# Gathers three tiles apart, slots placed earlier in the window, and a matmul for each gather to wait for

## The chip, the cores and the metric

The kernel runs on one core of a Trainium2 chip. The metric is the device time of one execution in microseconds; lower is better. Names of engines: PE is the matmul engine (PEld its weight loads), DVE the vector engine, ACT the scalar engine, POOL the GpSimd engine, SP the sync engine, which here only issues DMAs.

## What is computed

`x` has 16 batches of 512 tokens with 512 features, in float32. A conditional linear layer with a low-rank part gives g; a router picks 4 of 16 blocks of a feed-forward net for each token; the output is `x` plus the sum of the four blocks' results.

```python
z1 = einsum('bfi,bir->bfr', x, v) / 512
z = einsum('bfr,bor->bfo', z1, u) / 16             # u = v = fside
g = gelu(einsum('bfi,oi->bfo', x, W) + fc_bias + z + cond)
prob = softmax(g @ w_router + b_router)
_, idx = top_k(prob, 4)                            # 4 of 16 blocks for each token
h = relu(einsum('nd,ebd->neb', g, w1b) + b1b)      # block e: 128 hidden units
y = einsum('neb,ebd,ne->nd', h, w2b, mask) + b2
out = x + y
```

## The kernel before

**Lists in DRAM.** The kernel does the feed-forward only for the blocks that a token picked. Each block has a list of slots in DRAM, `g_d`, with room for a row of g in each slot. A token's g is scattered to four slots; tiles of 128 consecutive slots of one list are then computed; the results go to the same slots of `y_d`; and each token's four result rows are gathered back and added to x.

**Stage one, the windows.** `window(b)` runs for the 16 batches. It has eight halves (`cond_half(b, h)`), each with the `pc` matmuls (L261) of half an output quarter; after each second half `gelu` (ACT, L270) makes `gT`. The table `do` lists what is issued behind each half, in the order in which the engines get it, since PE, DVE and ACT follow the program's order: for the next batch `weights` (`pw` matmuls L241, four `we` adds on DVE L243) and `turn_x` (transposes L248, copy `xT` on DVE L250); for the batch before, called `a`, `logits_in` (`pa`, L285), `logits` (`pl`, L294), `route_in` (three small DVE operations and Exp on ACT), `route` (DVE: top 4, one-hot, counts), four `turn_g` (transposes L357, a copy `gr` on DVE L359 or ACT L361), `rank` (`pp` matmuls, L417 to L423) and `place`, which writes `slot`, the row numbers of a batch (L441). For the batch after next it has `spread_v`, `turn_v` and `turn_v_out`. Transposes share two PSUM buffers, `ps_t`; `pa`, `pl`, `pu` and `pp` share two others, `ps_s`. `chores` adds bookkeeping on DVE at halves 1, 3 and 6 of some windows: `fill`, `take`, `count`, `table_part`.

**The scatters.** `put(b, c, j, after)` (POOL, L447) scatters 128 rows of `gr` to the j-th choice's slots. There are 16 for a batch, two behind each half, for the batch two windows back, and each also waits for a matmul of that half. The last two batches' puts, and then five `put_zero` (L500) that fill up the last tile of each list, go into the first steps of stage two.

**Stage two, the tiles.** 271 tiles, one for each step `i`. SP: `fetch(i + 4)` loads `gt` (L631). PE, ACT: `turn(i + 1)` (transposes L649, copy `gs` on ACT L650), `first(i)` (`ph` L656, relu `h` on ACT L660), `second(i - 1)` (`py` L666, copy `y` on ACT L667, store to `y_d` on SP L668). DVE: `pick(i + 2)` copies the block's weights to `wcur` (L643), of which there are three. The first 22 tiles (`AHEAD`) are of full lists and don't wait for later scatters; tile 22 and those behind it wait for all puts and zeros.

**Sums.** A chunk is 128 tokens, 64 in all. `plan` puts its parts in steps: `load_x` (ACT's DMA queue, L689; chunks of the last two batches are still in SBUF) into one of 11 buffers; four `get_y` (POOL, L694), each a gather of 128 rows of `y_d`; then on DVE `sum_b` (L708), two `sum_y` (L712), two `sum_x` (L715); and `store` on SP (L718). `begun(b, c)` is the number of tiles that must be stored before the chunk is complete: 38 for the first five chunks, then 4n + 15 for the n-th. A gather waits for these stores. It also waits for its `yg` tile, of which there are six, for two gathers each. `mark[0]` is the last `ph` matmul issued. The planned step of a chunk's gathers is

```python
at = max(begun(b, c) + GAP, at + TOP_K if b + c else 0)     # GAP = 3, TOP_K = 4
```

so it is 41 for the first chunk, and 4n + 37 for the n-th: 293 for the last, 22 steps after the last tile.

Of the kernel before, what the change touches and what calls it, by code (L numbers as in the profile page):

```python
# [19 lines left out]
TOP_K = 4  # L20
# [5 lines left out]
def adaln_ffn_kernel(  # L26
# [31 lines left out]
    B, S, D = x.shape  # L58
# [3 lines left out]
    NC = S // P  # L62
# [27 lines left out]
    SYNC = mybir.DependencyInfo(mybir.DependencyClass.Sync, mybir.DependencyReason.DATA)  # L90

    def alone(ins):

        tc.declare_no_dep(ins.ins, group="put_g", reason="disjoint rows of the lists")
        tc.declare_no_dep(ins.ins, group="get_g", reason="the tiles that run ahead are full")
        tc.add_to_no_dep_group("put_g", ins.ins)
# [348 lines left out]
    def put(b, c, j, after):  # L445

        ins = nc.gpsimd.indirect_dma_start(  # L447
            out=g_d[:, :],
            out_offset=bass.IndirectOffsetOnAxis(ap=slot[:, b, c, j : j + 1], axis=0),
            in_=grs[b, c].bitcast(I32),  # L450
            in_offset=None,
        )
        tc.add_manual_dep(ins.ins, after.ins.name, SYNC, reason="spread over the products")
        alone(ins)
        if b < Q:
            early.append(ins.ins)
# [42 lines left out]
    def put_zero(i, after):  # L499
        ins = nc.gpsimd.indirect_dma_start(  # L500
            out=g_blocks if i else g_d[:, :],
            out_offset=bass.IndirectOffsetOnAxis(ap=zero_i[:, i : i + 1], axis=0),
            in_=(zero if i else zero[:, 0:D]).bitcast(I32),
            in_offset=None,
            bounds_check=NSLOT // ZB - 1 if i else NSLOT - 1,
            oob_is_err=False,
        )
        tc.add_manual_dep(ins.ins, after.ins.name, SYNC, reason="spread over the products")
        alone(ins)
# [65 lines left out]
    for k in range(known):  # L575
        chores.setdefault(B - 2 + k // 3, []).append(parts_of[k])

    def window(b):
        a = b - 1
        do = [[] for _ in range(2 * ND)]  # L580
        if b + 1 < B:
            do[0] += [(weights, b + 1)]
            do[2] += [(turn_x, b + 1, 0), (turn_x, b + 1, 1)]
            do[4] += [(turn_x, b + 1, 2), (turn_x, b + 1, 3)]
            if b > 0:
                do[1] += [(logits_in, a)]
                do[3] += [(logits, a), (route_in, a)]
                do[4] += [(route, a)]
                do[5] += [(turn_g, a, 0), (turn_g, a, 1)]
                do[6] += [(turn_g, a, 2), (turn_g, a, 3)]  # L590
                do[7] += [(rank, a), (place, a)]
            if b + 2 < B:
                do[2] += [(spread_v, b + 2)]
                do[5] += [(turn_v, b + 2), (turn_v_out, b + 2)]
        else:
            do[0] += [(logits_in, a)]
            do[1] += [(logits, a), (route_in, a)]
            do[2] += [(turn_g, a, 0), (turn_g, a, 1), (route, a)]
            do[3] += [(turn_g, a, 2), (turn_g, a, 3)]
            do[5] += [(rank, a), (place, a)]  # L600
        for h, what in zip((1, 3, 6), chores.get(b, ())):
            do[h] += [what]
        for h in range(2 * ND):
            ins = cond_half(b, h)
            for what, *args in do[h]:
                what(*args)
            if b > 1:
                for j in (0, 1):
                    put(b - 2, h // 2, h % 2 * 2 + j, ins)
            if later:  # L610
                what, *args = later.pop(0)
                what(*args)
# [4 lines left out]
    rows, gts, wcs, gss, hTs, mark, stores = {}, {}, {}, {}, {}, {}, []  # L617
# [59 lines left out]
    def begun(b, c):  # L677

        n = b * NC + c + 1
        return max(AHEAD + E, n * PB // NC + E - 1)  # L680
# [10 lines left out]
    def get_y(b, c, j):  # L691
        if j % 2 == 0:
            ygs[b, c, j // 2] = ygp.tile([P, 2, D], F32, tag="yg", name=f"yg_{b}_{c}_{j}")
        ins = nc.gpsimd.indirect_dma_start(  # L694
            out=ygs[b, c, j // 2][:, j % 2, :].bitcast(I32),
            out_offset=None,
            in_=y_d[:, :],
            in_offset=bass.IndirectOffsetOnAxis(ap=slot[:, b, c, j : j + 1], axis=0),
        )
        new = stores[begun(b, c - 1) if b + c > 0 else 0 : begun(b, c)]  # L700
        tc.declare_no_dep(ins.ins, group="put_y", keep=new, reason="later tiles have no slot of this chunk")
        for p in new:
            tc.add_manual_dep(ins.ins, p.name, SYNC, reason="its rows")
        tc.keep_in_program_order(ins)
        tc.add_to_no_dep_group("get_y", ins.ins)

# [14 lines left out]
    GAP = 3  # L721
# [4 lines left out]
    def plan(step, *what):  # L726
        work.setdefault(step, []).append(what)

    for b in range(B):
        for c in range(NC):  # L730
            at = max(begun(b, c) + GAP, at + TOP_K if b + c else 0)
            k = b * NC + c
            soon = FREE - 2 * XA + 2 * k if k < XA else FREE + 4 + k - XA
            plan(soon if k < XA + XB else max(at - 24, soon), load_x, b, c)
            for j in range(TOP_K):
                plan(at + j, get_y, b, c, j)
            plan(at + LAND, sum_b, b, c)
            for h in range(2):
                plan(at + LAND + 1 + 2 * h, sum_y, b, c, h)
                plan(at + LAND + 2 + 2 * h, sum_x, b, c, h)  # L740
            plan(at + LAND + 4, store, b, c)


    z = B - 1
    for step, *what in (
        (-1, logits_in, z), (0, logits, z), (0, route_in, z), (1, turn_g, z, 0), (1, turn_g, z, 1), (1, route_a, z),
        (2, route_b, z), (2, turn_g, z, 2), (3, route_c, z), (3, turn_g, z, 3), (4, rank, z), (5, place, z),
        (6, count, B // Q - 1), (7, ends), *((8 + k, *w) for k, w in enumerate(parts_of[known:])), (8 + NTC, table, 1),
    ):
        plan(step, *what)  # L750
    for i in range(NC * TOP_K):
        for k, b in enumerate((z - 1, z)):
            plan(8 * k + i // 2, lambda b, c, j: put(b, c, j, mark[0]), b, i // TOP_K, i % TOP_K)
    for i in range(1 + NZ):
        plan(16 + i // 3, lambda i: put_zero(i, mark[0]), i)

    ENG = mybir.EngineType
    with tc.manual_schedule(engines={ENG.PE, ENG.DVE, ENG.Activation}):
# [10 lines left out]
        for b in range(B):  # L769
            if 2 <= b + 2 < B:  # L770
                load(b + 2)
            window(b)
# [76 lines left out]
```

## Time and profile before

| what | value |
|---|---|
| median of 3 runs | 1096.34 us (1089.81 to 1098.36) |
| profiled execution | 1086.83 us, its span 1085.1 us |
| mean granted PE clock | 0.967 |
| busy: PE, DVE, ACT, POOL | 970.9, 648.0, 518.8, 550.3 us |
| DMA | 342.43 MB, 316 GB/s over the span |
| puts (L447), gathers (L694) | 256 each, 993 and 1106 ns on POOL |

The profile page splits the span into 40 slices of 27.1 us and gives the busy share of each engine in tenths. A group's row names line, engine, operation, output and input, count, then busy time and mean duration. A timeline row has the start and the length in us, engine, line, operation and tiles, and in brackets how long the engine had been idle before it and what ended that. A releaser called remote is another core or a queue that the profile doesn't know.

### The profile page before, as it was taken

What the parts mean: (1) busy time and instruction counts of PE and PEld (TensorE: products, weight loads), DVE (VectorE), ACT (ScalarE), POOL (GpSimd) and SP (SyncE); (2) the same over time, 40 slices, a digit from 0 to 9 for tenths busy, and PEclk for the clock granted to TensorE, in tenths of its full rate; (3) what the DMA queues carried; (4) which work ended last, traced back from release to release, by engine and by line L of the source; (5) the groups of instructions that cost most, each with busy time, mean ns of one, the idle gap of its engine ahead of it and who ended that gap; (6) DMA issues with size and microseconds to landing.
All of it is one profiled execution on the core that took longest, in us unless ns stands there. A gap on an engine that the chain in (4) does not pass through costs nothing.

```text
span 1085.1 us, 19007 instructions
## 1 busy us (share of the span) xinstructions
PE 970.9 (89%) x5320; PEld 639.3 (59%) x5320; DVE 648.0 (60%) x1450; ACT 518.8 (48%) x1006; POOL 550.3 (51%) x538
## 2 busy tenths in 40 slices
PE   5998988988999888789799999999999999999960
PEld 3544444544444455567577677677767777777740
DVE  4365667566556767323366666566666666666675
ACT  2333332342333434456466666566656566666640
POOL 2046666666666667500454445455444454444555
PEclk9999999999999988989899999999999999999985
DMA  9966667566654469988799999999999999999996
GB/s 301 332 230 216 224 215 261 208 225 242 226 223 179 170 224 318 358 265 272 259 382 405 394 388 403 391 394 395 395 397 401 395 396 398 380 405 398 392 354 211
DMA packets 161480, 342.43 MB, mean 316 GB/s; under 512 B 28723, under 2 KB 36951, under 8 KB 159046
## 3 DMA queue, kind: packets, MB, share of 16 engines
q1 hardware_dynamic: 110928, 188.53, 48.1%
q0 software_dynamic: 41856, 136.96, 33.6%
q10 hardware_dynamic: 8592, 15.73, 4.1%
q8 instruction: 44, 0.72, 0.3%
q14 instruction: 60, 0.49, 0.1%
HBM read 179.91 MB, written 163.32 MB: 316 GB/s over the span
## 4 chain that ended last, share of the span: by engine, by line
PE 58%; DMA 19%; DVE 8%; issue 5%; ACT 3%; POOL 2%; SPq 2%; another core or an unknown queue 2%; ACTq 1%; DVEq 0%; POOLq 0%
PE pc L261 17%; DMA gt<-g_d 14%; PE ph L656 14%; PE py L666 13%; PE pts L649 6%; PE ptx L248 2%; PE ptg L357 2%; PE pw L241 2%; PE pa L285 1%; ACT gs L650 1%; PE pl L294 1%; DVE xT L250 1%; DMA yg<-y_d,slot 1%; POOL g_d L447 1%
## 5 line engine op out<-in xcount | busy, mean ns | idle before, releaser
L694 POOL DMA_INDIRECT yg<-y_d,slot x256 | 283.1, 1106 | 338.0 <-DVE xr L715 163.8
L643 DVE COPY wcur<-wall 128x1028 f32 x271 | 193.0, 713 | 271.1 <-PE py L666 164.0
L447 POOL DMA_INDIRECT g_d<-gr,slot x256 | 254.3, 993 | 185.2 <-issue 65.8
L656 PE MATMUL ph<-gs,wcur 128*128 128x128 f32 x2168 | 293.7, 279 | 17.7 <-ACT gs L650 9.8
L666 PE MATMUL py<-wcur,h 128*128 128x512 f32 x542 | 281.2, 601 | 5.5 <-ACT h L660 4.8
L656 PEld LDWEIGHTS ph<-gs,wcur 128*128 128x128 f32 x2168 | 266.8, 194 | 26.6 <-ACT gs L650 17.4
L261 PE MATMUL pc<-xT,we 128*128 128x512 f32 x512 | 246.3, 608 | 0.0
L649 PEld LDWEIGHTS pts<-ident,gt 128*128 128x128 f32 x1084 | 134.9, 143 | 165.2 <-issue 108.8
L667 ACT COPY y<-py 128x512 f32<-128x512 f32 x271 | 159.2, 587 | 94.0 <-PE py L666 69.5
L650 ACT COPY gs<-pts 128x512 f32<-128x512 f32 x271 | 160.0, 590 | 85.0 <-DMA gt<-g_d 39.6
L649 PE MATMUL pts<-ident,gt 128*128 128x128 f32 x1084 | 165.6, 276 | 16.4 <-DMA gt<-g_d 14.3
L660 ACT ACTIVATE h<-ph,wcur 128x128 f32<-128x128 f32 x271 | 100.0, 369 | 89.6 <-PE ph L656 43.0
L261 PEld LDWEIGHTS pc<-xT,we 128*128 128x128 f32 x512 | 88.4, 192 | 88.7 <-issue 88.7
L270 ACT ACTIVATE gT<-pc,biasT 128x512 f32<-128x512 f32 x64 | 44.0, 688 | 158.0 <-PE pc L261 101.8
L712 DVE TENSOR_TENSOR yg<-yg 128x512 f32<-128x512 f32 x128 | 87.3, 682 | 8.2 <-DMA yg<-y_d,slot 6.8
L666 PEld LDWEIGHTS py<-wcur,h 128*128 128x128 f32 x542 | 83.2, 194 | 6.8 <-ACT h L660 5.1
L250 DVE COPY xT<-ptx 128x512 f32<-128x512 f32 x64 | 42.0, 686 | 60.4 <-PE ptx L248 27.8
L715 DVE TENSOR_TENSOR xr<-xr,yg 128x512 f32<-128x512 f32 x112 | 76.6, 684 | 0.0
L357 PE MATMUL ptg<-ident,gT 128*128 128x128 f32 x256 | 37.8, 281 | 27.1 <-issue 9.8
L357 PEld LDWEIGHTS ptg<-ident,gT 128*128 128x128 f32 x256 | 30.0, 143 | 50.5 <-issue 24.9
L243 DVE TENSOR_TENSOR we<-pw,wc 128x512 f32<-128x512 f32 x64 | 40.1, 683 | 23.9 <-PE pw L241 16.2
L248 PEld LDWEIGHTS ptx<-ident,x 128*128 128x128 f32 x256 | 31.3, 146 | 18.3 <-issue 14.9
(159 smaller groups left out, 511.2 us busy)
## 6 DMA issues: line engine op xcount, KB each, us to landing
gt<-g_d SPq DMA_DIRECT2D x271, 256.0 KB
y_d<-y SPq DMA_DIRECT2D x271, 256.0 KB
x<-in_x_dram SPq DMA_DIRECT2D x16, 1024.0 KB
xr<-in_x_dram ACTq DMA_DIRECT2D x56, 256.0 KB
out_dram<-xr SPq DMA_DIRECT2D x56, 256.0 KB
wall<-in_w1T_dram SPq DMA_DIRECT2D x16, 256.0 KB
wall<-in_w2T_dram SPq DMA_DIRECT2D x16, 256.0 KB
g_d<-gr,slot POOLq DMA_INDIRECT x256
```

Of the source, the lines that this page charges most:

```text
L261: ins = nc.tensor.matmul(pms[o], lhsT=wes[b][:, k, o * P : (o + 1) * P], rhs=xTs[b, k], start=(k == 0), stop=(k == ND - 1))
L357: nc.tensor.transpose(pt[:, k, :], gTs[b, k][:, c * P : (c + 1) * P], ident)
L447: ins = nc.gpsimd.indirect_dma_start(out=g_d[:, :], out_offset=bass.IndirectOffsetOnAxis(ap=slot[:, b, c, j : j + 1], axis=0), in_=grs[b, ...
L643: nc.vector.tensor_copy(wcs[i], wall_f[:, bass.DynSlice(w, WW)])
L649: nc.tensor.transpose(pt[:, k, :], gts[i][:, k * P : (k + 1) * P], ident)
L650: nc.scalar.copy(gs.rearrange("p k t -> p (k t)"), pt.rearrange("p k t -> p (k t)"))
L656: mark[0] = nc.tensor.matmul(ph, lhsT=wcs[i][:, k * P : (k + 1) * P], rhs=gss[i][:, k, :], start=(k == 0), stop=(k == ND - 1))
L660: nc.scalar.activation(h, ph, AF.Relu, bias=wcs[i][:, ND * P : ND * P + 1])
L666: nc.tensor.matmul(py, lhsT=hTs[i], rhs=wcs[i][:, ND * P + 4 : WW], start=True, stop=True)
L667: nc.scalar.copy(y, py)
L694: ins = nc.gpsimd.indirect_dma_start(out=ygs[b, c, j // 2][:, j % 2, :].bitcast(I32), out_offset=None, in_=y_d[:, :], in_offset=bass.Indir ...
L712: nc.vector.tensor_tensor(yg[:, 0, :], yg[:, 0, :], yg[:, 1, :], ALU.add)
```

## The change

Four things are edited. In `window` the table `do` is one for all windows: `logits_in` of batch `a` moves from half 1 to 0, `logits` and `route_in` from 3 to 1, `route` from 4 to 2, `rank` and `place` from 7 to 4; `turn_g` goes to halves 4, 6, 7 and 7; `weights` from 0 to 3; `turn_x` to halves 1, 5, 5 and 6. The puts run ten behind (`LAG`): in window b the last ten of batch b - 2 and then the first six of batch b - 1, and the last ten of batch 14, the 16 of batch 15 and the zeros take steps 0 to 4, 6 to 13 and 14 of stage two. The chunks come three steps apart until 3n + 38 meets 4n + 18 at the 20th chunk (step 98), and from there `at` is `begun + 3`: 274 for the last chunk. A chunk's four gathers stand at `at`, `at`, `at + 1` and `at + 2`. Last, each gather also waits for `mark[0]`, the `ph` matmul of its step.

```diff
--- before.py
+++ after.py
@@ -575,38 +575,38 @@
     for k in range(known):
         chores.setdefault(B - 2 + k // 3, []).append(parts_of[k])
 
+    LAG = 10
+
+    def puts_of(b, i, after):
+        if b >= 0:
+            put(b, i // TOP_K, i % TOP_K, after)
+
     def window(b):
         a = b - 1
         do = [[] for _ in range(2 * ND)]
-        if b + 1 < B:
-            do[0] += [(weights, b + 1)]
-            do[2] += [(turn_x, b + 1, 0), (turn_x, b + 1, 1)]
-            do[4] += [(turn_x, b + 1, 2), (turn_x, b + 1, 3)]
-            if b > 0:
-                do[1] += [(logits_in, a)]
-                do[3] += [(logits, a), (route_in, a)]
-                do[4] += [(route, a)]
-                do[5] += [(turn_g, a, 0), (turn_g, a, 1)]
-                do[6] += [(turn_g, a, 2), (turn_g, a, 3)]
-                do[7] += [(rank, a), (place, a)]
-            if b + 2 < B:
-                do[2] += [(spread_v, b + 2)]
-                do[5] += [(turn_v, b + 2), (turn_v_out, b + 2)]
-        else:
+        if b > 0:
             do[0] += [(logits_in, a)]
             do[1] += [(logits, a), (route_in, a)]
-            do[2] += [(turn_g, a, 0), (turn_g, a, 1), (route, a)]
-            do[3] += [(turn_g, a, 2), (turn_g, a, 3)]
-            do[5] += [(rank, a), (place, a)]
+            do[2] += [(route, a)]
+            do[4] += [(rank, a), (place, a), (turn_g, a, 0)]
+            do[6] += [(turn_g, a, 1)]
+            do[7] += [(turn_g, a, 2), (turn_g, a, 3)]
+        if b + 1 < B:
+            do[1] += [(turn_x, b + 1, 0)]
+            do[3] += [(weights, b + 1)]
+            do[5] += [(turn_x, b + 1, 1), (turn_x, b + 1, 2)]
+            do[6] += [(turn_x, b + 1, 3)]
+        if b + 2 < B:
+            do[2] += [(spread_v, b + 2)]
+            do[5] += [(turn_v, b + 2), (turn_v_out, b + 2)]
         for h, what in zip((1, 3, 6), chores.get(b, ())):
             do[h] += [what]
         for h in range(2 * ND):
             ins = cond_half(b, h)
             for what, *args in do[h]:
                 what(*args)
-            if b > 1:
-                for j in (0, 1):
-                    put(b - 2, h // 2, h % 2 * 2 + j, ins)
+            for i in range(2 * h, 2 * h + 2):
+                puts_of(b - 2 + (i >= LAG), (i - LAG) % (NC * TOP_K), ins)
             if later:
                 what, *args = later.pop(0)
                 what(*args)
@@ -701,6 +701,7 @@
         tc.declare_no_dep(ins.ins, group="put_y", keep=new, reason="later tiles have no slot of this chunk")
         for p in new:
             tc.add_manual_dep(ins.ins, p.name, SYNC, reason="its rows")
+        tc.add_manual_dep(ins.ins, mark[0].ins.name, SYNC, reason="spread over the products")
         tc.keep_in_program_order(ins)
         tc.add_to_no_dep_group("get_y", ins.ins)
 
@@ -728,12 +729,12 @@
 
     for b in range(B):
         for c in range(NC):
-            at = max(begun(b, c) + GAP, at + TOP_K if b + c else 0)
+            at = max(begun(b, c) + GAP, at + 3 if b + c else 0)
             k = b * NC + c
             soon = FREE - 2 * XA + 2 * k if k < XA else FREE + 4 + k - XA
             plan(soon if k < XA + XB else max(at - 24, soon), load_x, b, c)
             for j in range(TOP_K):
-                plan(at + j, get_y, b, c, j)
+                plan(at + 3 * j // TOP_K, get_y, b, c, j)
             plan(at + LAND, sum_b, b, c)
             for h in range(2):
                 plan(at + LAND + 1 + 2 * h, sum_y, b, c, h)
@@ -748,11 +749,12 @@
         (6, count, B // Q - 1), (7, ends), *((8 + k, *w) for k, w in enumerate(parts_of[known:])), (8 + NTC, table, 1),
     ):
         plan(step, *what)
+    for i in range(LAG):
+        plan(i // 2, lambda i: puts_of(z - 1, i, mark[0]), NC * TOP_K - LAG + i)
     for i in range(NC * TOP_K):
-        for k, b in enumerate((z - 1, z)):
-            plan(8 * k + i // 2, lambda b, c, j: put(b, c, j, mark[0]), b, i // TOP_K, i % TOP_K)
+        plan(6 + i // 2, lambda i: puts_of(z, i, mark[0]), i)
     for i in range(1 + NZ):
-        plan(16 + i // 3, lambda i: put_zero(i, mark[0]), i)
+        plan(14, lambda i: put_zero(i, mark[0]), i)
 
     ENG = mybir.EngineType
     with tc.manual_schedule(engines={ENG.PE, ENG.DVE, ENG.Activation}):
```

## Prediction

> **What bounds the kernel now.** I read the page's slices first, then busy time by stretches, the waits, and the timeline of each engine.
>
> ```profile
> PE   5998988988999888789799999999999999999960
> POOL 2046666666666667500454445455444454444555
> DMA  9966667566654469988799999999999999999996
> GB/s 301 332 230 216 224 215 261 208 225 242 226 223 179 170 224 318 358 265 272 259 382 405 394 388 403 391 394 395 395 397 401 395 396 398 380 405 398 392 354 211
> ```
>
> A slice is 27.1 us. Up to slice 15 (stage one, the windows) PE is busy and DMA is not full. From slice 21 on PE and DMA are both at 9 and the rate stays near 396 GB/s. In the last slices PE is gone: a tail of POOL, DVE and DMA.
>
> ```profile
> 459.00:486.00 27.00, 20.66 (x126) 16.23 (x127) 5.58 (x8) 12.54 (x26) 0.00 (x0) 0.83 0.76 248
> 513.00:540.00 27.00, 19.06 (x106) 14.03 (x105) 8.30 (x13) 10.74 (x23) 13.10 (x14) 0.81 0.78 260
> 702.00:729.00 27.00, 26.47 (x169) 19.91 (x168) 17.48 (x27) 16.98 (x36) 13.29 (x12) 1.00 1.04 393
> 1053.00:1080.00 27.00, 0.00 (x0) 0.00 (x0) 18.46 (x29) 0.00 (x0) 18.07 (x17) 0.50 0.85 271
> ```
>
> These stretches (PE, PEld, DVE, ACT, POOL busy, then clock, DMA share, GB/s) show three places where PE loses time besides the full-DMA stretch: about 460, about 525, and after 1053. The start of each tile's relu (ACT L660, in ACT's timeline) numbers the tiles: tile 0 at 393.18, 20 at 455.73, 21 at 468.23, 41 at 512.10, 43 at 518.27, 44 at 529.75, 270 at 1048.06. Where nothing disturbs, one tile takes 2.19 us (22 to 42): PE's own pace. From 74 to 242 it takes (986.28 - 596.92) / 168 = 2.318 us.
>
> ```profile
> PE ptg L357 <- issue: 7.9, 5, 1.8
> PE ptg L357 <- DVE gr L359: 7.4, 4, 2.1
> PE ptg L357 <- ACT gr L361: 2.8, 1, 2.8
> ```
>
> These are PE's waits in 100 to 343 us (total, times, longest): in stage one nearly all are at the transposes of g (L357).
>
> **Stage one: the new order in a window.** From rank matmul to rank matmul (L423) windows 2 to 14 take 22.9, 24.6, 22.2, 25.3, 24.9, 22.2, 23.3, 25.3, 22.4, 23.6, 23.7, 25.2 and 24.0 us, 309.6 together. The shortest three, less the 0.8 to 1.0 us that PE waits in each, give 21.4 us of work, so 31 us are lost. The loss has one form: the third and fourth `turn_g` (half 6) need a `ps_t` buffer whose copy `gr` (DVE) stands behind `route`, 4.35 us of DVE work issued at half 4 (334.94 to 339.28).
>
> I walk one new window with the rows of the old one, from the start of half 0: 1.8 us for the four pc matmuls of a half, pa 1.0, pl 0.8, four transposes 0.44, pw 1.1, rank 0.3. pa ends at 2.8 and pl at 5.4; `route_in` (three ops of 0.22) 6.2; Exp, with its table load of 1.28 behind gelu at half 1, 7.0; `route` on DVE 7.1 to 11.4; PE comes to `rank` at 12.35, 0.9 later, so no wait. The `we` adds take DVE to 13.9, `place` to 15.45. The next users of `ps_t`: `turn_g(0)` at 12.65 wants the first `we` add (12.1); `turn_x(1)`, `turn_x(2)` at 14.9 and 15.35 want 12.7 and 13.8; `turn_g(1)` at 18.05 wants 16.1; `turn_g(2)`, `turn_g(3)` at 20.75 and 21.2 want 19.3 and 20.0. Nothing waits. I take 0.3 us for each of the seven plain windows, where 12.9 are lost now: -10.8.
>
> In the six windows with chores (5, 6, 7, 9, 13, 14) the move costs something: `count` at half 1 (4.1 us of DVE, 231.62 to 235.83) now stands before `route`, so acc comes at about 15.3 and `rank` waits 2.9 us; a `table_part` (2.5 us) does the same in smaller. I charge 2.2 to 3 us each, 16.7, where 18.5 are lost now: -1.8. Window 15 gets a `rank` wait of 2.3 us, but PE waits there 2.23 us for `wcur` before its first tile anyway: 0. **Stage one: about -12**; bounds 0 (every margin missed) and -25 (no chore window waits).
>
> **The scatters into stage two.** A put is 0.97 us and 0.30 between two, 1.27. Six puts of the last batch but one now go out in window 15, POOL having 20.4 us of puts per window, under its length. After stage one 10 + 16 + 5 DMAs remain instead of 32 + 5. The last puts are gated by steps 6 to 13, the zeros by step 14 (440.9). `slot` of the last batch is written at 414.2, before step 6 (415.9). So the zeros start at 441.3 instead of 448.31, 7 us sooner.
>
> ```profile
> 453.96 1.05 POOL L500 DMA_INDIRECT g_d<-zero,zero_i  x1 [0.31 <-issue]
> 465.34 1.09 PE L649 MATMUL pts<-ident,gt 128*128 128x128 f32 x4 [10.14 <-DMA gt<-g_d]
> ```
>
> The last zeros land at 462.5; SP then issues gt of tile 22, and its transposes stop waiting: the 12.5 us between tiles 20 and 21. At most 10.3 can go. DMA is full there (share 1.0 from 441 to 453), and six puts of 262 KB less at 370 GB/s are 4.2 us. **I take -5**, between 0 and -10.
>
> **The gathers, from tile 41 on.** Now POOL issues twelve gathers in a row (512.3 to 527.5) until the six `yg` tiles are full.
>
> ```profile
> 529.74 0.70 DVE L643 COPY wcur<-wall 128x1028 f32 x1 [9.36 <-remote]
> 529.75 0.37 ACT L660 ACTIVATE h<-ph,wcur 128x128 f32<-128x128 f32 x1 [6.53 <-remote]
> ```
>
> Behind the burst tiles 43 and 44 take 3.98 and 11.48 us: 11.1 lost. The releaser is unknown; it stands nowhere else at that length, so I tie it to the burst. With a product of its own step for each gather there is no burst, and the 11.1 go (they are in the sum below). Behind a waiting gather POOL has only more gathers; who waits for them is DVE's sums.
>
> Against that stand bytes. A tile moves 0.262 MB of gt and as much of y; each gather 0.262, each xr load and out store 0.262 per chunk. One chunk per four tiles makes 0.918 MB, over 2.318 us 396 GB/s: the limit. From steps 41 to 98 a chunk now comes every three tiles.
>
> - Before: 41 to 61 (no xr loads) 20 x 2.19, the loss 11.1, 61 to 237 176 x 2.318, then no loads, 33 x 2.19: 535.2 us. The trace has 535.96.
> - After: 41 to 50 at 2.21 and out stores from 48, 20.3; 50 to 74 with 1.049 MB, 24 x 2.648 = 63.6; 74 to 98 with 1.027 MB, 24 x 2.593 = 62.2; 98 to 218 as now, 278.2; the loads end 19 steps sooner, 52 x 2.19 = 113.9. Sum 538.2: **+3**.
>
> The Trainium skill ("DMA: Bandwidth & Descriptors", Where 436 GB/s comes from) speaks otherwise on both sides: the ports give 435 GB/s, while for HBM to SBUF some 358 per core bind. By 435 the stretch 98 to 218 would be PE's (2.19), and the difference -2; by 358 it is +5. The row of 396 is between and decides.
>
> Two waits are added. (a) An xr load goes to one of 11 buffers, and is planned 24 steps ahead. With chunks 33 steps apart instead of 44 over 11 chunks it comes 9 steps after the old owner's gathers, 2 after its out store. That store is issued about 2.5 us after its step's relu and lands some 7 us later (605.35, 7.02 in the chain), so ACT, at 6.8 us, stands about 2.7 us in front of the load; gs of the next tiles is queued behind it, and PE for gs. gs has 1.3 us of slack (514.0 against 515.34). Some ten loads: 0 if the full DMA hides it, 14 beyond the slack, 27 with none. I take +4, near the low end, as PE waits 0.4 us per tile for gt there anyway.
>
> (b) From step 98 on a gather stands three steps behind its last tile. That tile's y leaves 2.3 us after the relu of the next step; gt in the same queue lands in 6.6 to 8.4 us when DMA is full, so the stores are there 2.4 us after the gather's own product. POOL then starts two gathers, the second 3.7 us after that relu. The sum that reads them stands on DVE at 10.9 (four steps, and 1.6), before the copies of `wcur`, for which PE waits. So 7.2 us are left for landing. Rows: 4.4 to 5.8 in the tail, when 271 to 354 GB/s flow; gt's 8.4 at the other end. The same page (Arbitration) has each DMA engine go round its rows by packets, so gathers, in a row of their own, don't queue behind SP's; I take 5.5, nearest the tail's, and 0 for the wait. At 8.4 it is 1.2 us, of which 1.1 is slack.
>
> **The tail.** Now from relu 270 to the end 37.0 us: 21 gathers at 1.3 and the last one's way out. After, eight gathers are left; those of the last chunk wait for y of tile 270: issued at 2.7, landed 5.2 later (the way from about 507 to 512.3 that the first gather waits for today), 7.9; four gathers, last start 11.8, landed 16.9; two adds 18.3; store 3.7 (1081.4 to 1085.1): 22.0. **-15.**
>
> **Sum:** -12 - 5 + 3 + 4 - 15 = **-25**. The profiled execution (span 1085.1, time 1086.83) would take 1061.8. It ran 9.5 below the median 1096.34; on that I forecast **1071**. A measurement of this kernel can tell about 1% from no change.
>
> **Rivals.**
> 1. The waits are only moved (within 1%, chance 0.17): stage one gives 3 for 12, since `rank` now stands close behind `route`, the scatters' stall is DMA's (0), and ACT pays 10 for 4: -3 +3 +10 -15 = -5, 1091. For it: margins of 0.5 to 0.9 us in my walk, full DMA at 447 to 453. Against: three windows of 22.2 to 22.4 today.
> 2. Slower (0.18): sums in wait of gathers. From chunk 20 on, 44 chunks; it begins where a gather lands later than 7.2 + 1.1 = 8.3 us after its start and costs 44 us per us. At 9.2 it is +40: 1071 + 40 = 1111. For it: DVE is in order and `wcur` stands behind; stores to HBM at full DMA could take longer than gt. Against: 4.4 to 5.8 in the tail.
> 3. More (0.10): stage one gives 25 and the scatters 10, ACT nothing: -25 -10 +3 -15 = -47, 1049.
>
> My forecast has 0.55. Faster 0.55 + 0.10, same 0.17, slower 0.18. The likeliest case alone runs from 1055 to 1085; the range, with most of rival 1 and 3 and part of 2, from 1048 to 1106.
>
> **What would show it.** Rank to rank near 21.7 in plain windows and about 24 in those with `count`, no 1.8 us waits at L357; zeros near 7 us sooner against relu 14; no jump at tiles 43 and 44; 2.6 us per tile from 50 to 98 at 396 GB/s; ACT waiting for out stores before L689; no DVE wait for `yg` over 2 us; 22 us from relu 270 to the end. Wrong if tiles 98 to 218 take more than 2.4 us, or windows over 23.

## Result: slower, and by how much depends on the chip

| chip | before | after | ratio (95% interval) |
|---|---|---|---|
| the chip of the times shown above | 1095.48 us (6 runs) | 1135.12 us (6 runs) | 1.0359 (1.0303 to 1.0416) |
| a second chip, later | 1060.21 us (7 runs) | 1076.06 us (4 runs) | 1.0153 (1.0116 to 1.0189) |

The change makes the kernel slower. The forecast was 1071 us, with a range from 1048 to 1106, on the first chip. The experiments met five chips. On one of them before takes about 1094 us, as on the first (it may be the same chip); on the other four 1059 to 1062 us. I call them chips of the first and of the second kind. The trace shows the difference too: in all six traces of the first kind, 9 to 21 waits (27 to 56 us in all) end with a releaser called remote, and in all fourteen of the second kind none does.

The name misleads here. An engine tells another that its work is done by raising a counter, a semaphore, and the trace records each increment. All 93 of these waits end with an increment of one semaphore (117), which only PE's own instructions raise. So no other core stands behind them: PE's signal came later than the end that the profile gives its matmul, and that end is modelled. The six traces also lack 41 to 45% of the increments that the program's DMAs should leave, the fourteen at most 0.5%. So on the first kind the names of releasers are less certain than on the second.

From the start of each tile's relu, the parts of the time are as follows, in us. For before on the second kind I use e4, which differs from it only in what the puts wait for and takes the same time (0.9994).

| part | before, 1st | after, 1st | before (e4), 2nd | after, 2nd | forecast of the change |
|---|---|---|---|---|---|
| start to tile 0 | 393.2 | 437.5 | 377.2 | 387.2 | -12 |
| tile 0 to 41 | 118.9 | 113.2 | 115.9 | 109.0 | -5 |
| 41 to 98 | 141.0 | 150.8 | 131.9 | 150.4 | |
| 98 to 218 | 279.5 | 282.0 | 281.0 | 280.9 | 41 to 270 together: |
| 218 to 270 | 115.4 | 118.3 | 115.7 | 118.1 | +3 +4 |
| tile 270 to the end | 37.0 | 25.3 | 37.6 | 25.2 | -15 |
| span | 1085.1 | 1127.2 | 1059.3 | 1070.8 | -25 |

On the first kind the sum is +44.3 -5.7 +15.2 -11.7 = +42.1; on the second +10.0 -6.9 +20.8 -12.4 = +11.5. What was to be gained at tiles 20 to 22 and in the tail is there. What was lost lies in stage one and in tiles 41 to 98.

The same slices, stretches and lines as shown of before, now from after on the first chip. A slice is 28.2 us here.

```profile
PE   5996988798998879779987999999999999999991
POOL 2046655565666556620354454444544444544443
DMA  9965655574755347978899999999999999999995
GB/s 302 337 209 191 216 183 194 204 247 148 259 209 214 147 153 228 323 280 305 268 358 393 362 397 402 394 391 404 399 387 399 400 390 391 394 398 348 388 354 187
```

Stage one (to slice 15) has one slice at 6 and one at 7 where, behind the first slice, before had only 8 and 9. At the end PE is at 9 until the last slice but one: the tail is shorter.

```profile
498.00:525.00 27.00, 22.64 (x134) 17.05 (x133) 6.29 (x10) 14.06 (x29) 0.00 (x0) 0.94 0.76 260
553.00:580.00 27.00, 22.88 (x141) 17.15 (x140) 14.44 (x22) 14.48 (x31) 15.18 (x15) 0.97 1.01 369
740.00:767.00 27.00, 26.06 (x165) 19.46 (x164) 16.52 (x26) 17.13 (x37) 12.82 (x12) 1.00 1.04 392
1100.00:1127.00 27.00, 3.29 (x13) 1.39 (x12) 10.22 (x16) 2.03 (x5) 9.68 (x10) 0.64 0.56 188
```

The columns are again PE, PEld, DVE, ACT, POOL busy, clock, DMA share, GB/s. PE gets 2 us more in the first stretch (tiles 20 to 22) and nearly 4 more in the second, where the gathers begin; the third is as before. Line by line:

```profile
486.19 0.98 POOL L500 DMA_INDIRECT g_d<-zero,zero_i  x1 [0.31 <-issue]
503.83 1.09 PE L649 MATMUL pts<-ident,gt 128*128 128x128 f32 x4 [4.36 <-DMA gt<-g_d]
555.91 0.70 DVE L643 COPY wcur<-wall 128x1028 f32 x1 [1.49 <-PE py L666]
557.29 0.37 ACT L660 ACTIVATE h<-ph,wcur 128x128 f32<-128x128 f32 x1
```

The last zero stands 5.8 us behind the relu of tile 14, where it stood 13.1 behind; PE's wait at tile 22 falls from 10.14 to 4.36 us. At tiles 43 and 44 no wait of 9.36 and 6.53 us is left. The transposes of g hardly wait in this stretch any more (5.6 us in all, 22.1 before); rank does (PE's waits from 100 to 343 us: total, times, longest):

```profile
PE pp L417 <- DVE acc L350: 15.7, 7, 5.2
PE pw L241 <- DVE xT L250: 3.2, 3, 1.1
PE ptg L357 <- DVE xT L250: 2.9, 2, 1.9
```

### The profile page after: what moved, and what is told of

It is laid out like the page before. It is cut to its first block, busy times and chain, and to the rows that moved or that the text cites. A ratio compares the mean times of both kernels' runs of the same rounds, so it can differ in the third digit from the quotient of the medians.

```text
span 1127.2 us, 19110 instructions
## 1 busy us (share of the span) xinstructions
PE 991.4 (88%) x5320; PEld 648.0 (57%) x5320; DVE 643.8 (57%) x1450; ACT 517.1 (46%) x1006; POOL 539.1 (48%) x538
## 4 chain that ended last, share of the span: by engine, by line
PE 72%; DVE 10%; DMA 9%; issue 4%; ACT 2%; SPq 1%; ACTq 1%; another core or an unknown queue 0%; POOL 0%; DVEq 0%; POOLq 0%
PE ph L656 18%; PE pc L261 18%; PE py L666 17%; PE pts L649 9%; DMA gt<-g_d 4%; DMA out_dram<-xr 3%; PE ptg L357 3%; PE ptx L248 3%; PE pa L285 1%; PE pl L294 1%; ACT gs L650 1%; PE pw L241 1%; DVE ti L326 1%; DVE we L243 1%; DVE xT L250 1%
## 5 line engine op out<-in xcount | busy, mean ns | idle before, releaser
L694 POOL DMA_INDIRECT yg<-y_d,slot x256 | 273.8, 1070 | 357.2 <-DMA y_d<-y 113.1
L643 DVE COPY wcur<-wall 128x1028 f32 x271 | 193.8, 716 | 241.6 <-PE py L666 143.7
L656 PEld LDWEIGHTS ph<-gs,wcur 128*128 128x128 f32 x2168 | 266.6, 194 | 44.9 <-ACT gs L650 29.1
L261 PE MATMUL pc<-xT,we 128*128 128x512 f32 x512 | 252.8, 625 | 0.0
L261 PEld LDWEIGHTS pc<-xT,we 128*128 128x128 f32 x512 | 93.6, 200 | 101.6 <-issue 94.7
L300 DVE TENSOR_TENSOR pr<-pl,br 128x64 f32<-128x64 f32 x16 | 3.6, 225 | 108.7 <-PE pc L261 60.5
L361 ACT COPY gr<-ptg 128x512 f32<-128x512 f32 x32 | 18.6, 583 | 85.0 <-PE ptg L357 74.1
```

The lines of the kernel that those rows point to most:

```text
L261: ins = nc.tensor.matmul(pms[o], lhsT=wes[b][:, k, o * P : (o + 1) * P], rhs=xTs[b, k], start=(k == 0), stop=(k == ND - 1))
L643: nc.vector.tensor_copy(wcs[i], wall_f[:, bass.DynSlice(w, WW)])
L656: mark[0] = nc.tensor.matmul(ph, lhsT=wcs[i][:, k * P : (k + 1) * P], rhs=gss[i][:, k, :], start=(k == 0), stop=(k == ND - 1))
L694: ins = nc.gpsimd.indirect_dma_start(out=ygs[b, c, j // 2][:, j % 2, :].bitcast(I32), out_offset=None, in_=y_d[:, :], in_offset=bass.Indir ...
```

## Experiments

Two theories of stage one came out of the two first traces. **U**: when POOL issues a long unbroken row of puts, releases reach ACT and DVE late. **R1**: the new order makes PE wait at rank, because work on DVE stands ahead of the route. This is what led to U, from after on the first chip; two rows of POOL, one of ACT, one of PE:

```profile
68.86 0.97 POOL L447 DMA_INDIRECT g_d<-gr,slot  x1 [5.34 <-DVE acc L350]
93.21 0.97 POOL L447 DMA_INDIRECT g_d<-gr,slot  x1 [0.30 <-issue]
94.49 0.59 ACT L289 COPY parts<-pa 128x512 f32<-128x512 f32 x1 [13.57 <-remote]
95.13 1.89 PE L294 MATMUL pl<-pick,parts 128*128 128x16 f32 x8 [11.69 <-issue]
```

Twenty puts stand in a row from 68.9 to 94.2. `pa` is complete at 81.5, yet its copy on ACT begins at 94.49, when the row ends; PE stands 11.69 us behind it. In the same window on the second kind (after_again) the copy begins when `pa` ends:

```profile
81.49 0.59 ACT L289 COPY parts<-pa 128x512 f32<-128x512 f32 x1 [2.48 <-PE pa L285]
```

In eleven of the twelve windows that follow in after, the chain from `pa` to `route_in` is late by 0.6 to 3.2 us against after_again.

**e1 to e4 (second kind).** The two halves of the change alone, the old places of the puts in the new window, and a row of puts in the old window.

```diff
 e1 = before
+            at = max(begun(b, c) + GAP, at + 3 if b + c else 0)
+                plan(at + 3 * j // TOP_K, get_y, b, c, j)
+        tc.add_manual_dep(ins.ins, mark[0].ins.name, SYNC, reason="spread over the products")
 e2 = after without these three
 e3 = after
-    LAG = 10
+    LAG = 16
 e4 = before
-            if b > 1:
-                for j in (0, 1):
-                    put(b - 2, h // 2, h % 2 * 2 + j, ins)
+            if b > 1 and h == 0:
+                for j in range(NC * TOP_K):
+                    put(b - 2, j // TOP_K, j % TOP_K, ins)
```

> The kernel before with the gathers' part of the change alone: chunks three tiles apart, and each gather waits for its tile's product. Stage one is that of before, so tile 0's relu should start at 393 us in every theory. If the two traces add up part by part, tiles 41 to 270 take some 551 us instead of 536 and the end behind the last relu 25 instead of 37: the kernel lands at about +3 us, 1099. The rival that the gathers gain by themselves what the prediction gave them (+7 there, -15 at the end) says 1087. If the wait for the product is what hurts, tiles 41 to 270 take over 555 us and it is slower than 1105.

> The changed kernel with the gathers of before (four tiles apart, no wait for a product), so the windows' new order and the puts' new places alone. Both theories of the windows say that tile 0's relu starts at about 437 us, 44 later than before, and that tiles 0 to 41 give 6 back: about 1133 us. If instead the gathers' part carries the loss, this one is at 1100 or less.

> The changed kernel with LAG = 16 instead of 10: the order of work in a window stays new (rank right behind route), but all 16 puts of a batch stand two per half in the window after its slots are known, as before, so GpSimd never waits for slots and then catches up. Theory U (a long unbroken row of puts on GpSimd makes the releases of the scalar and the vector engine late by 1 to 3 us, on the chain from logits to rank): windows of 22 to 23.5 us, tile 0 at 385 to 400 us, total about 1093 (stage one back, tiles 0 to 41 keep or lose the 6 us that the earlier puts gained). Rival R1 (the new order itself lets TensorE wait for the route's sums at rank): windows stay at 24 to 25 us, tile 0 at 425 to 437, total 1125 to 1140.

> The kernel before, with one edit: the 16 puts of a window all wait for the first half's product instead of two for each half, so that GpSimd issues them in one row of some 20 us; nothing else moves. Theory U: the logits of the next batch lie within that row, their releases come 1 to 3 us late in two or three places, and windows grow by 2 to 5 us, tile 0 at 420 to 450 us, total 1120 to 1150. Rival R1 (order of work only): windows unchanged at 22 to 25 us, tile 0 at 390 to 398, total 1090 to 1100.

Before took 1061.4 us here. Measured: e1 1072.5 (1.0106, 1.0053 to 1.016), e2 1064.2 (1.0035, 1.0021 to 1.0049), e3 1085.4 (1.0206, 1.014 to 1.0272), e4 1060.3 (0.9994, 0.9975 to 1.0012). Against my expectation the gathers' part carries most of the loss on this chip: e1's tile 0 is at 376.3, but tiles 41 to 270 take 551.7 us where e4 takes 528.6, and 12.7 come back in the tail. The window part is +10 us at tile 0 (387.7), not +44. And U fails here: e4's puts stand in unbroken rows of 20 us, and its plain windows are 22.2 us all the same. e3, with two puts behind each half again as in before, is no help either; its windows are those of e2.

What is left of the window's loss shows in windows counted from the last gelu of one batch to that of the next (windows 1 to 15, from ACT's timeline, us):

| | 1 | 2 | 3 | 4 | 5 | 6 | 7 | 8 | 9 | 10 | 11 | 12 | 13 | 14 | 15 |
|---|---|---|---|---|---|---|---|---|---|---|---|---|---|---|---|
| e4 (old) | 21.9 | 22.1 | 22.2 | 22.2 | 24.9 | 24.2 | 22.2 | 22.2 | 22.2 | 22.2 | 22.2 | 22.2 | 22.2 | 21.7 | 17.9 |
| e2 (new) | 20.2 | 21.1 | 21.1 | 21.1 | 24.5 | 26.2 | 26.3 | 21.1 | 26.3 | 21.1 | 21.1 | 21.1 | 26.1 | 24.4 | 21.9 |
| e7 (new, chores late) | 20.2 | 21.1 | 21.1 | 21.1 | 21.1 | 21.1 | 21.1 | 23.0 | 21.1 | 22.8 | 21.1 | 21.1 | 21.1 | 22.3 | 18.8 |

The seven plain windows gain 1.1 us each, window 1 gains 1.7: 9.4 together. The seven with chores (5, 6, 7, 9, 13, 14, 15) lose 20. One of them, window 7 of e2, on DVE and then on PE:

```profile
184.48 0.43 DVE L388 TENSOR_TENSOR first_q<-first_q,left 128x256 f32<-128x256 f32 x1
184.83 0.21 DVE L318 TENSOR_REDUCE sm<-ex 128x4 f32<-128x64 f32 x1
188.44 0.77 DVE L350 TENSOR_TENSOR acc<-acc,mask 128x16 bf16<-128x16 bf16 x4
189.26 0.20 PE L417 MATMUL pp<-acc,ones 128*128 128x80 bf16 x1 [2.81 <-DVE acc L350]
190.63 3.30 PE L261 MATMUL pc<-xT,we 128*128 128x512 f32 x4
```

```profile
187.00:189.20 2.20, 0.00 (x0) 0.00 (x0) 1.96 (x10) 0.00 (x0) 1.59 (x3) 1.00 0.48 181
190.60:193.80 3.20, 3.20 (x7) 1.31 (x6) 2.36 (x8) 0.59 (x1) 0.00 (x0) 0.55 0.08 28
```

`count` holds DVE from 180.85 to 184.83, and `route` begins the moment it ends. So rank waits 2.81 us, and that is not all: from 190.6 to 193.8 the granted clock is 0.55, and the four `pc` matmuls that take 1.88 us elsewhere take 3.30. Window 7 is 5.2 us over a plain one: PE stands still for 3.15 us of it, and its work takes 2.03 us longer. This is R1, with a price nearly twice the wait.

**after_again, e5, e6, e7 (second kind).** The changed kernel itself; the spacing without the wait for a product; the sums two steps later; the chores behind rank.

```diff
 e5 = e1
-        tc.add_manual_dep(ins.ins, mark[0].ins.name, SYNC, reason="spread over the products")
 e6 = e1
-    LAND = 3
+    LAND = 5
 e7 = e2
-        for h, what in zip((1, 3, 6), chores.get(b, ())):
+        for h, what in zip((5, 6, 7), chores.get(b, ())):
```

> The changed kernel itself, beside the next three on one chip. If its loss of 3.6% belongs to the program, it is 3 to 4% slower than before wherever it runs. If the late releases (44 us in stage one, up to 3 us behind each long row of puts) belong to the state of the chip that the first runs were made on, then on a chip where before takes about 1061 us the parts add up: windows +3 us, gathers +11 us, about +14 us or 1.3%.

> The kernel before with chunks three tiles apart and without the wait for a product. If the wait for the product makes the loss of the gathers' part (a gather can't start until its tile's product, so it lands later and the vector engine waits for it), tiles 41 to 270 take 520 to 535 us here and the end stays short (25 us): 5 to 15 us faster than before. If the spacing makes it (gathers, tiles and stores crowd together from the start), it is as e1: about 11 us slower.

> e1 (before with the gathers' part, wait for the product included) with LAND = 5 instead of 3: the sums of a chunk are placed two tiles later, nothing else. If the loss comes from the vector engine waiting at the sums for gathers that have not landed (66 us of such waits in e1, 49 times), these waits fall below 15 us, tiles 41 to 270 take 525 to 535 us instead of 549, and it is 8 to 15 us faster than e1, at or below before. If it comes from the transfers' rate, it stays at e1's time (+1%).

> The new window with the gathers of before (as e2), and the counting work of the chores at halves 5, 6 and 7 instead of 1, 3 and 6, so behind rank and not ahead of route on the vector engine. If the chores ahead of route are what eats the shorter windows, all windows but the two with the first counts take 21.1 us, the three count windows lose their 5 us, the last two 3 to 4 each: tile 0 at 365 to 372 us on a chip as quiet as the last, total 15 to 20 us under e2 and 12 to 18 under before. If the new order itself makes TensorE wait at rank, windows with a count stay at 24 to 26 us and the total at e2's.

Measured, with before at 1060.2: after 1076.1 (1.0153), e5 1074.2 (1.0144, 1.0089 to 1.02), e6 1117.0 (1.0523, 1.0482 to 1.0564), e7 1042.7 (0.9834, 0.9797 to 0.9871).

The parts add up in after. e5 is where e1 was, so the added wait for a product costs nothing that these runs can tell, and the spacing is what costs. e6 does not settle what the sums cost: DVE's waits for gathers did fall, from 66 to 10 us, but a longer wait came in their place, and the kernel became 44 us slower. Two lines, the first of e1 and the second of e6 (total, times, longest):

```profile
DVE yg L713 <- DMA yg<-y_d,slot: 66.2, 49, 6.0
```

```profile
ACT gs L650 <- DMA out_dram<-xr: 62.0, 10, 7.4
```

With the sums later a chunk gives its x buffer back later, and the load of x for a later chunk, planned 24 steps ahead, stands on ACT until then. `gs` is queued behind it. That is the wait (a) of the prediction, and it shows what it can cost once the two steps of margin are gone (tiles 41 to 98 take 197.9 us, 53 more than in e1); in after it is 11.6 us in 3 waits (14.8 in 5 on the first chip).

e7 shows R1: the same window with the chores moved behind rank has 21.1 us in ten of the windows 2 to 14, and it reaches tile 0 at 362.4, 25 us before e2. PE's waits at rank, first in after on this chip and then in e7:

```profile
PE pp L417 <- DVE acc L350: 12.9, 6, 2.8
```

```profile
PE pp L417 <- DVE acc L350: 0.7, 1, 0.7
```

e7 beats both kernels on this kind of chip.

**e8 to e11 (first kind; before 1093.5).** The chores alone in the old window; the loads of x at 16 steps in e1; before without the loads of x; the changed kernel with the chores late.

```diff
 e8 = before, e11 = after
-        for h, what in zip((1, 3, 6), chores.get(b, ())):
+        for h, what in zip((5, 6, 7), chores.get(b, ())):
 e9 = e1
-            plan(soon if k < XA + XB else max(at - 24, soon), load_x, b, c)
+            plan(soon if k < XA + XB else max(at - 16, soon), load_x, b, c)
 e10 = before
-        if b >= B - KEPT:
-            xrs[b, c] = xs[b][:, c, :]
+        if True:
+            xrs[b, c] = xs[B - KEPT + b % KEPT][:, c, :]
```

> The kernel before with its chores at halves 5, 6 and 7 instead of 1, 3 and 6, and nothing else. If the place of the chores is worth something by itself, the two long windows (25 and 24 us) fall to 22.2 and the total is 4 to 6 us under before. If it only pays together with the new window (rank at half 4, so that the chores can come behind it), it is within 3 us of before; a chore that now stands ahead of rank at half 7 may even cost 2 to 3 us in each count window, so up to 8 slower.

> e1 (before with the gathers' part) with each load of x planned 16 steps ahead of its chunk instead of 24. With chunks three tiles apart a buffer of 11 comes free some 26 steps ahead, so a load at 24 can stand on the scalar engine waiting for a store to end. If these waits make the catch-up slow, the waits of gs for the output's store vanish, tiles 41 to 98 take 5 to 8 us less than in e1 and the total is 4 to 8 us under e1's +1%. If the transfers' rate alone makes it, no change: within 3 us of e1.

> The kernel before without the loads of x in stage two: every chunk adds the two kept batches' x in place of its own, so the output is not the reference's; gathers, sums and stores stay. It asks whether stage two of before is bound by the transfers. They move 0.92 MB for each tile there while chunks follow four tiles apart, at 393 GB/s 2.33 us; without x 0.85 MB, 2.17 us, under TensorE's 2.19. If the transfers bound, tiles 98 to 218 take 263 to 268 us instead of 281, tiles 41 to 98 125 to 127 instead of 132, and the total falls by 20 to 28 us. If it is waits from engine to engine, both stay and the total falls by less than 5.

> The changed kernel with one edit: the chores at halves 5, 6 and 7, behind rank. If windows and gathers add up, it gains 25 us on the changed kernel in stage one (as e7 on e2) and keeps the gathers' loss of 10 to 15: 1050 to 1056 us where before takes 1060, about half a per cent faster than before and slower than e7. If the loss of the gathers' part hung on the late windows, it is at e7's 1043 or below.

Measured: e8 1100.2 (1.0065, 1.0036 to 1.0094), e9 1095.9 (1.0004, 0.9974 to 1.0034), e10 1066.4 (0.976, 0.9708 to 0.9811), e11 1121.4 (1.0259, 1.0208 to 1.0309).

e10 answers what bounds stage two. Tiles 98 to 218, first of e4 (before, second kind), then of e10:

```profile
625.00:906.00 281.00, 272.73 (x1680) 198.68 (x1680) 174.84 (x271) 170.36 (x361) 136.15 (x120) 1.00 1.04 393
```

```profile
647.53:910.43 262.90, 262.90 (x1681) 199.65 (x1680) 177.41 (x270) 173.58 (x361) 132.74 (x121) 1.00 1.03 390
```

Take 7% of a tile's bytes away and the 120 tiles take 262.9 us, 2.19 each; PE is busy in every one of these microseconds. So in before the transfers bound these tiles, at 393 GB/s. (Tiles 41 to 98 of e10 take 133.0 us, not the 125 to 127 expected; 8.1 of it is the hole at tiles 42 to 45 that before has on this kind of chip.) With that the gathers' part can be read. Tiles 41 to 98, e4 and then after on a chip of the second kind:

```profile
493.05:625.00 131.95, 128.99 (x804) 94.61 (x802) 81.53 (x126) 82.01 (x172) 72.83 (x64) 1.00 1.03 390
```

```profile
496.25:646.64 150.39, 132.56 (x799) 98.11 (x798) 96.22 (x145) 81.64 (x172) 79.58 (x76) 0.97 1.02 377
```

POOL starts 76 gathers here instead of 64, and four x loads and four output stores more go with them: 20 x 0.262 = 5.2 MB, of which 4.3 MB are gone from the tail. At 390 GB/s they take 13.4 us, and 12.4 us is what the tail got shorter. Transfers moved from idle queues to full ones cost about what they saved. The other 5.0 of the 18.4 us are rate: 377 GB/s where before had 390. The shortfall lies in tiles 50 to 74 (370 GB/s, 404 in e4), where two of the three waits of ACT before the x loads stand (7.8 of 11.6 us).

e9 leaves this as it is: `gs` waits only 1.2 us for output stores (4.1 in e1), and tiles 41 to 98 take 144.5 us (144.8). Its rate there is 391 GB/s, that of before, where e1 had 385; but e1 had little of that wait to lose, and e9 moves more bytes in the stretch (56.5 MB, 55.8). So that wait (a) makes the lower rate is likely, not shown. That e9 equals before here and e1 did not says nothing of the loads: on this kind of chip before has its hole at tiles 43 to 45 (11 us on the first chip; e8 8.66 us at tile 44 here), and e9 has not.

e8 and e11 ran into the first kind's late signals. e8's +6.7 us lies within its widest expectation (up to 8 slower), e11 missed its own by far. e8's windows lie anywhere from 22.2 to 26.4 us, with 56 us of remote waits in the trace, so its +0.65% says nothing sure of the chores. e11 has lost R1's waits (rank 6.8 us in all, against 28.0 in after), and it reaches tile 0 at 420.1, 17.4 us sooner than after; but its windows stay at 23.7 to 25.8, not 21.1, and its window 3 is 36.7 us:

```profile
99.03 0.58 ACT L289 COPY parts<-pa 128x512 f32<-128x512 f32 x1 [13.59 <-remote]
```

It is the same copy, at the same place behind a row of puts, that stood 13.57 us in after; the row had ended 3.2 us earlier here. On the second kind window 3 takes 21.1 us with the same instructions: e7, whose stage one is that of e11, reaches tile 0 57.7 us earlier.

**e12 to e17 (meant for the first kind, met the second; before 1061.7 and 1059.2).** e12 and e16 are e7 again, e13 is e4 again. e14 and e15 (and e17, which is e15 again) are e7 with puts of 64 columns, and without the puts of 14 batches. Their tiles are read from x at fixed rows, so they don't compute the reference's output, and only their windows are compared.

```diff
 e14, e15 = e7 (fetch)
-        ins = nc.sync.dma_start(out=gts[i].bitcast(I32), in_=g_d[bass.DynSlice(rows[i], T), :])
+        ins = nc.sync.dma_start(out=gts[i].bitcast(I32), in_=x_v[i // NC % B][:, i % NC, :].bitcast(I32))
 e14 (put)
-            out=g_d[:, :],
+            out=g_d.rearrange("n (k f) -> (n k) f", f=64),
...
-            in_=grs[b, c].bitcast(I32),
+            in_=grs[b, c][:, 0:64].bitcast(I32),
 e15 (puts_of)
-        if b >= 0:
+        if b >= B - 2:
```

> e7 once more (new window, chores behind rank, gathers of before). On a quiet chip 1.7% faster than before, windows of 21.1 us. On a chip where before takes about 1094 us: if the late releases come with GpSimd's unbroken rows of puts, which at 1.27 us each fill 20.4 of a window's 21.1 us, windows come out at 24 to 25 us, one of them at 36, and it is 1 to 2% slower than before; if they were a matter of the gathers' part, it is 1 to 2% faster there too.

> The kernel before with the 16 puts of a window in one row (e4) once more. On a quiet chip no change, as e4. On a chip with before at 1094: theory U (rows on GpSimd make the releases late there) says that windows grow by 1 to 4 us against before's 22 to 25, tile 0 at 410 to 440 us, 2 to 4% slower; if rows do not matter, it is within 1% of before there too.

> e12 with puts of 64 columns instead of 512 (same number of instructions on GpSimd, an eighth of the bytes), and tiles read from x at fixed rows, so what the tiles compute is not the reference's. Windows are what counts. On a chip with before at 1094: if the number of puts in a row makes the late releases, windows stay at 24 to 25 us as in e12; if the bytes that the puts write make them, windows fall to 21.1 to 22. On a quiet chip 21.1 in both.

> e12 with the puts of 14 batches left out (those of the last two stay) and tiles read from x at fixed rows, so what the tiles compute is not the reference's. Windows are what counts. On a chip with before at 1094: if GpSimd's puts make the late releases, windows fall to 21.1 us, all of them, tile 0 near 362; if they come from elsewhere (x loads, code, the chip), windows stay at 23 us and more. On a quiet chip 21.1.

> The best version (new window, chores behind rank, gathers of before) a third time. On a quiet chip 1.7% faster than before. On a chip where before takes about 1094 us: with theory U windows of 24 to 25 us and 1 to 2% slower than before; if the late releases belonged to the gathers' part, 1 to 2% faster.

> The same without the puts of 14 batches and with tiles read from x at fixed rows, so what the tiles compute is not the reference's. On a chip where before takes about 1094 us: theory U says windows of 21.1 to 22 us, tile 0 near 362 to 370; if something else on that chip makes the releases late, 23 us and more, tile 0 at 390 to 420. On a quiet chip 21.1 us, as in e15.

Measured: e12 1043.8 (0.983, 0.9809 to 0.985), e16 1041.2 (0.9823, 0.9775 to 0.987), e13 1060.7 (0.9987, 0.9976 to 0.9998), e14 1035.9, e15 1038.0 and e17 1035.2 (one run each). Window 7 of e12, e14 and e15:

```profile
161.60:182.70 21.10, 21.05 (x95) 10.69 (x93) 17.48 (x63) 8.11 (x13) 15.91 (x18) 1.00 0.88 320
```

```profile
161.80:182.90 21.10, 21.05 (x95) 10.70 (x93) 17.51 (x63) 8.10 (x13) 15.92 (x18) 1.00 0.25 79
```

```profile
161.70:182.80 21.10, 21.10 (x95) 10.76 (x93) 17.19 (x63) 8.11 (x12) 0.00 (x0) 1.00 0.16 50
```

With 320, 79 or 50 GB/s, with 18 puts on POOL or none, the window is 21.10 us and PE is busy in all of it. On the second kind of chip the puts cost a window nothing, whatever their form. The question these runs were meant for stays open.

## Why the prediction was wrong, step by step

**Stage one: -12 forecast, +10 and +44 measured. This step failed.** The walk through a plain window was right: it found 0.3 us over 21.4 us of work, and the new plain windows take 21.1. Two terms were mis-sized and one was missing.
- What the old windows lose was read from one trace as a property of the program: 12.9 us in seven plain windows and 18.5 in six with chores. On the second kind the old plain window is 22.2 us, so 1.1 us each were to be gained, 7.7 in all, and only windows 5 and 6 had more to give. (With 1.7 from window 1, which the forecast left out, that makes 9.4 us; that it is near the 10.8 is luck.) The rest of the old loss is met on the first kind alone, and the new order does not remove it: on the first chip the seven plain windows came out 10.5 us longer (11.1 of it in window 3), the six with chores 29.1 and window 15 8.3.
- The chores ahead of `route` were seen ("rank waits 2.9 us"; measured 2.81) and charged 2.2 to 3 us. The wait was right and the price wrong: 5.2 us over a plain window, since the clock drops behind it, and window 15, charged nothing, cost 4.0, of which only 1.0 came back as a shorter wait for `wcur`. On the second kind the six chore windows came out 16 us worse than the old ones, not 1.8 better.
- On the first kind come 34 us more than on the second (44 against 10): at tile 0 before is 16 us over its time on the second kind, after 50. PE's late signals are what the traces show in their place. The chain from `pa` to `route_in`, batches 0 to 14, is late by 38.8 us in all in after (against after_again) and by 16.5 in before (against e4). The waits called remote alone don't show it: up to tile 0 they are 20 us in after and 29 in before. Nothing in the forecast stood for that, and its own alarm, windows over 23 us, was met.

**The scatters: -5 forecast, -5.7 and -6.9 measured. Right**, and by the step given: zeros 7.2 us sooner, the stall at tile 22 shorter by 5.8.

**The gathers: +3 forecast from tile 41 to 270 with the waits +4; measured +15.2 and +20.8. Half right.** For tiles 41 to 98 of after the byte sum and the wait (a) say 146.1 + 4 = 150.1, and the traces have 150.8 and 150.4. Wait (b) was put at 0, with 5.5 us for a gather to land; on the second kind they land in 6.6 us in the median (59 gathers of tiles 98 to 218), hardly sooner than gt (7.0), so a row of their own hardly spares them the full queues; and DVE does wait for them (88 us in 57 waits, up to 4.8). Yet tiles 98 to 218 of after take 280.9 and 282.0 us, as before: the transfers bound there, and the waits stand in their shadow. So the rival that made this wait a loss of 40 us falls too. That it costs nothing is not shown: e1 and e3, with the same gathers, take 290.8 and 287.0 us there. Two terms failed. The last 52 tiles were to run at PE's 2.19 us (113.9) and take 118. And the hole of 11.1 us was counted as the old program's: it is gone in after, as forecast, but before has it only on chips of the first kind. On the second kind nothing stands against the 18.5 us.

**The tail: -15 forecast, -11.7 and -12.4 measured. Right in kind**; the last stretch takes 25.3 us instead of 22.0.

The rival that ends slower was looked for in stage two, in the sums. The loss came in stage one, and the part of it that is explained comes from a wait that the text itself had listed.

**What stays open.** Why PE's signals reach ACT and DVE late on the first kind, and whether the increments that its traces lack have the same cause. The longest of these waits go with long rows of indirect DMAs on POOL: 13.57 and 13.59 us with 20 puts, 9.36 with 12 gathers, and they end 0.3, 3.2 and 2.2 us behind the row. Many shorter ones end close behind rows of 7 to 10. But the rows alone do not do it: on the second kind rows as long do nothing. Whether shorter rows would help on the first kind was not shown, as no run of e13 to e17 met such a chip; nor was e7 run on one. With e11 at +2.6% there, its 1.7% must not be taken for granted on the first kind.

## To carry to other kernels

Before a stretch of lost time in a profile is counted as gain, ask whether the program alone made it: where a wait has no releaser in the program, or one called remote, profile the same program on a second chip first. Here all such waits were gone there, and with them the 16 us by which stage one of before is longer on the first. When a chain is pulled forward in an in-order queue, move what stands ahead of it on that queue too: here a one-line move of the bookkeeping from ahead of the route to behind rank turned +0.35% into -1.7%. And moving transfers from the end into a stretch where the queues are full only moves the time; count the bytes of the stretch they go to.

## What the hardware showed that I had not expected

The granted clock changes only at the borders of windows of 3.41 us: every stretch of low clock in stage one is one or several of them, at 0.50. What counts is how much of one such window PE stands still, not how long a wait is. Two pairs from e2, each a window and the one behind it:

```profile
142.28:145.70 3.42, 1.65 (x10) 1.23 (x11) 3.35 (x8) 0.41 (x1) 2.51 (x4) 1.00 0.50 192
145.70:149.11 3.41, 3.41 (x16) 1.85 (x14) 1.38 (x3) 1.35 (x3) 2.80 (x3) 1.00 1.02 281
166.18:169.59 3.41, 1.55 (x10) 0.83 (x9) 3.27 (x12) 0.00 (x0) 2.72 (x3) 1.00 0.73 237
169.59:173.00 3.41, 3.41 (x7) 1.41 (x6) 1.33 (x3) 0.60 (x1) 2.50 (x4) 0.50 1.02 347
```

In the first pair PE waits 2.82 us, but a border parts the wait, 1.77 us of it fall into this window, and the clock stays. In the second it waits only 1.86 us, all in one window, and the clock halves. In the eleven traces of the second kind with a low window in stage one, all 22 windows with more than 1.9 us of standing still were followed by a low one, and none of the 1024 with less than 1.7 (on the first kind 22 of 22, and 3 of 579). Behind the four longest waits at rank in e2 (2.60 to 2.81 us) the next four `pc` matmuls took 2.78 to 3.54 us instead of 1.88. The Trainium skill ("TensorE: Matmul & The Clock Gate", The HAM clock gate) gives an idle window of about 3.4 us for this; here just over half of such a window sufficed.

The same program differs by 3% in time from chip to chip (before 1060 and 1094 us), and the changed one by 5% (1076 and 1135). A likely reason, not tested: in the new plain windows PE has no idle time left (0.00 us in e2, some 0.75 in the old ones of e4), so they have less slack for a late signal.
